# Dealing a table's tiles out over fewer edge groups in two layers of a graph network

## The chip, the cores and the metric

The program runs on one core of one Trainium2 chip. The metric is the time of one execution on the device, in microseconds (us). Three runs of the kernel before took 9591.27, 9617.38 and 9623.91 us; the median, 9617.38 us, stands for it.

## What is computed

Four layers of a graph network on 12,500 nodes of 128 features and 212,500 edges that are sorted by destination. Each layer normalises the nodes, applies a ReLU, gathers the rows of the edges' sources, combines them per destination and adds the result to x:

```python
h = relu(layernorm(x)); x = x + L0(h)   # attention over the incoming edges, GELU, layer norm
h = relu(layernorm(x)); x = x + L1(h)   # L1 = gelu(gelu(segment_sum(h[src] * w, dst)) @ W.T + b)
h = relu(layernorm(x)); x = x + L2(h)   # equivariant products per edge, summed per destination
h = relu(layernorm(x)); x = x + L3(h)   # mean of relu(h)[src] per destination, two matmuls, batch norm
```

Only layers 1 and 3 are touched by the change.

## The kernel before

Edges are cut into 208 groups of 1024: 128 partitions by T = 8 slots. For a slot, an indirect DMA on POOL's queue fetches 128 source rows, one on each partition. A one-hot matrix, made by DVE, says to which of 128 consecutive destinations each row goes, and a matmul on PE adds the rows up in PSUM. We call these eight matmuls of a group the group matmuls.

In layers 1 and 3 the destinations are split. The first 56 blocks of 128 nodes are served in this way, by the first G0 = 121 groups. The other NW = 42 blocks (windows) need no gather: the whole table of rows is loaded into SBUF once (tabS), and each window goes through NT = 26 **tiles**. A tile picks 128 rows out of the table with four matmuls by one-hot weights (out px), ACT copies px to SBUF (out xs, or xb in layer 3), and one matmul scatters them onto the window's 128 nodes (out pw). That is 42 x 26 = 1092 tiles in each of the two layers.

The tiles of layer 1 are written by the generator tabled1 (lines 1210 to 1295), those of layer 3 by tabled (from line 1465). Each resumption of the generator issues one tile; both generators have two resumptions ahead of the first tile, and that of layer 1 has one more at the end of each window. For every seven tiles or fewer the generator also issues an SP load of the tile's indices (lob) and two DVE instructions that make the one-hot matrices (oha, ohb), and for every window one small gather on POOL (xo). px has two buffers.

The order of work is written out by hand (manual_schedule). A loop counts rounds g. Round g issues on POOL the gathers of group g, on DVE its one-hot matrix, and on PE the eight group matmuls of group g - 1. After each of these eight, a formula says how many resumptions are due, and the generator is resumed until that many are done. In layer 1 (lines 1346 to 1349):

```python
goal = total * (T * (g - first) + t + 1) // (T * (last_ - first + 1))
while alive and count < min(goal, total + T + NW):
    alive = next(windows1, "end") != "end"
    count += 1
```

Layer 3 (lines 1637 to 1640) has the same formula with the limit total + T. total is 1092, first is 6 in layer 1 and 10 in layer 3, and last_ is G0 - 1 = 120 in both (lines 1311 and 1593). Rounds go on after the last group until everything else is done.

The gathered rows lie in rings: 96 buffers in layer 1 (twelve groups, line 1329), 28 in layer 3 (three and a half groups, xg). A gather waits until the group matmul that read its buffer is done.

Nodes are finished in batches of four blocks, by generators that are stepped once in a round. In layer 1 node1 (lines 603 to 624) has five steps: GELU, a matmul (L617), a bias (L620) and GELU (L621), the sum (L623) and statistics, then the normalised rows, which are stored to htab. The batch of the last gathered blocks (number 13) starts at round 123, and that of the last windows (number 24) when they are done. Layer 2 gathers from htab, so its first gather waits for the last store. In layer 3 node3 (lines 658 to 686) takes seven steps for a batch of gathered blocks and five for a batch of windows, one batch at a time; those that wait are run off after the last group. A batch norm over all nodes and the output follow.

Of the kernel before, what the change touches and what calls it, by code (L numbers as in the profile page):

```python
# [93 lines left out]
def gnn_kernel(ctx: ExitStack, tc, x, src, dst, ef16, ef9, ew, W0, We0, a0, lns, lnb, W1, b1,  # L94
# [13 lines left out]
    G0 = E * W0_ * P // (N * GE) + 2  # L108
# [15 lines left out]
    def load_edges(t, v, g0, g1, fill, k):  # L124

        full = min(g1, NF)
        if full > g0:
            nc.sync.dma_start(
                t[:, : full - g0, :],
                v[g0 * GE * k : full * GE * k].rearrange("(g p t) -> p g t", p=P, t=T * k))  # L130
        if g1 > NF:
            j, e0 = NF - g0, NF * GE
            rp, rem = divmod(tail, T)
            pool.memset(t[:, j, :], fill)
            if rp:
                nc.sync.dma_start(t[:rp, j, :], v[e0 * k : (e0 + rp * T) * k].rearrange("(p t) -> p t", t=T * k))
            if rem:
                nc.sync.dma_start(t[rp : rp + 1, j, : rem * k], v[None, (e0 + rp * T) * k : E * k])
# [464 lines left out]
    def node1(sp, pp, k, held=None):  # L603
        b0, nb = k * NBK, min(NBK, NB - k * NBK)
        xv = sp.tile([P, nb, D], F, name="xv")
        load_rows(xv, xtab[0], b0, nb)
        g = sp.tile([P, nb, P], F, name="g")
        if held is None:
            settle(k)
        act.activation(g.rearrange("p j n -> p (j n)"),  # L610
                       acc.t[:, cols(k)] if held is None else held[:, : nb * P], AF.Gelu_apprx_tanh)
        yield
        if held is None:
            vec.memset(acc.t[:, cols(k)], 0.0)
        po = pp.tile([P, nb, D], F, name="pn")
        for j in range(nb):
            pe.matmul(po[:, j, :], g[:, j, :], W1T, start=True, stop=True)  # L617
        yield
        o = sp.tile([P, nb, D], F, name="o")
        vec.tensor_tensor(o, po, b1_b[:, None, :].to_broadcast([P, nb, D]), ALU.add)  # L620
        act.activation(o, o, AF.Gelu_apprx_tanh)  # L621
        yield
        vec.tensor_tensor(xv, xv, o, ALU.add)  # L623
        yield from keep(sp, 1, k, xv, True)
# [142 lines left out]
    def gather_apart(take, table, idx):  # L767

        ts = []
        for s in range(T):  # L770
            ts.append(take())
            pool.indirect_dma_start(out=ts[-1][:, : table.shape[1]], out_offset=None, in_=table[:, :],  # L772
                                    in_offset=bass.IndirectOffsetOnAxis(ap=idx[:, s : s + 1], axis=0))
        return ts

    def one_hot(sp, r, wgt=None, dt=F):
        s = sp.tile([P, T, W], dt, name="oh")
        if wgt is None:
            vec.tensor_tensor(s, iop[:, None, :].to_broadcast([P, T, W]), r[:, :, None].to_broadcast([P, T, W]),
                              ALU.is_equal)  # L780
        else:
            for t in range(T):
                vec.tensor_scalar(s[:, t, :], io, r[:, t : t + 1], wgt[:, t : t + 1], op0=ALU.is_equal, op1=ALU.mult)
        return s
# [512 lines left out]
    with (tc.tile_pool(name="t1", bufs=1) as tp, tc.tile_pool(name="e1", bufs=3) as sp,  # L1297
          tc.tile_pool(name="e1p", bufs=2, space=PSUM) as pp,
          tc.tile_pool(name="n1", bufs=2) as ns, tc.tile_pool(name="n1p", bufs=2, space=PSUM) as np_):
        eww = tp.tile([P, NG, T], F, name="eww")  # L1300
        tabS = tp.tile([P, NB, P], F, name="tabS")
        vec.memset(tabS[:, NB - 1 :, :], 0.0)
        for g0 in (0, 16):
            load_edges(eww[:, g0 : 16 if g0 == 0 else NG, :], ew.rearrange("e o -> (e o)"), g0, 16 if g0 == 0 else NG,
                       0.0, 1)
        reg = Window(DVE, True)
        pag = pp.tile([P, 2, W], F, name="pag", bufs=1)
        S, pags, X, here, there = {}, {}, {}, [], []
        waiting = []
        windows1 = tabled1(sp, pp, tabS, lambda k, held: waiting.append((k, held)))  # L1310
        first, last_ = 6, G0 - 1
        total = NW * NT
        nk, count, alive = 0, 0, True
        with tc.manual_schedule():
            g = -1
            while g < G0 + 4 or alive or here or there or waiting:
                g += 1
                if 0 <= g - 2 < G0:
                    win = ds(reg.load(bir[0:1, g - 2 : g - 1], RW - 1), W)
                    reg.end(vec.tensor_tensor(acc.t[:, win], acc.t[:, win], pags.pop(g - 2), ALU.add))  # L1320
                if nk < W0_ // NBK and min(done[nk], G0 - 1) + 3 <= g:
                    here.append(node1(ns, np_, nk))
                    nk += 1
                if not there and waiting:
                    there = [node1(ns, np_, *waiting.pop(0))]
                here = [w for w in here if next(w, "end") != "end"]
                there = [w for w in there if next(w, "end") != "end"]
                if g < G0:
                    X[g] = gather_apart(lambda: sp.tile([P, D], F, name="X", bufs=96), htab[0], si[:, g, :])
                    S[g] = one_hot(sp, relx[:, g - G0 + GM, :] if g >= G0 - GM else rel[:, g, :], eww[:, g, :])  # L1330
                if g == 0:
                    full = NB - (LR < P)
                    for b in range(0, full, 14):
                        n = min(14, full - b)
                        nc.sync.dma_start(tabS[:, b : b + n, :],
                                          htab[0][b * P : (b + n) * P, :].rearrange("(j p) d -> p j d", p=P))
                    if full < NB:
                        nc.sync.dma_start(tabS[:LR, full, :], htab[0][full * P :, :])
                h = g - 1
                if 0 <= h < G0:  # L1340
                    p = pags[h] = pag[:, h % 2]
                    s, r = S.pop(h), X.pop(h)
                for t in range(T):
                    if 0 <= h < G0:
                        pe.matmul(p, r[t], s[:, t, :], start=t == 0, stop=t == T - 1)  # L1345
# [4 lines that stand above are left out]
# [222 lines left out]
    with tc.tile_pool(name="l3", bufs=1) as lp:  # L1572
        acc.t, acc.ring = lp.tile([P, AW], F, name="acc3"), None
        stats = lp.tile([P, NK, 6], F, name="stats")
        with (tc.tile_pool(name="t3", bufs=1) as tp, tc.tile_pool(name="e3", bufs=2) as sp,
# [14 lines left out]
            reg3 = Window(DVE, True)  # L1590
            X, S, sums, flat3, going = {}, {}, {}, {}, []
            nodes_at = [min(d, G0 - 1) + 6 for d in done[: W0_ // NBK]]
            first, last_ = 10, G0 - 1
            total = NW * NT
            with tc.manual_schedule():
                vec.memset(tabS[:, NB - 1 :, :], 0.0)
# [260 lines left out]
```

## Time and profile before

| what | value |
|---|---|
| median of three runs | 9617.38 us |
| profiled execution, its own time | 9495.71 us |
| its span in the trace | 9493.9 us |
| PE busy, share of the span | 5094.6 us, 54% |
| DVE busy | 5342.1 us, 56% |
| POOL busy | 5141.2 us, 54% |
| ACT busy | 2810.9 us, 30% |
| layer 1: first group matmul, last tile, first gather of layer 2 | at 3302.8, 5005.1, 5024.5 us |
| layer 3: first group matmul, last group matmul, last batch of nodes | at 7831.7, 9395.2, 9446 us |

The profile page gives each engine's busy time over the whole span and, in its second part, a row of 40 digits for each engine: the busy share of each fortieth of the span (237 us) in tenths. PEclk in these rows is the clock that PE was granted, in tenths of the full one. The view by stretches gives the same for any stretch of time: busy us and, in brackets, the number of instructions of each engine, then the granted clock and the DMA's share. A timeline gives single instructions in order of time: start, duration, engine, line, what it writes and reads, how many were merged, and in square brackets how long the engine was idle before and what ended that. In layer 1 a matmul in f32 shows as two instructions.

### The profile page before, as it was taken

How to read it: one execution, taken by the hardware profiler on the slowest of the kernel's cores; microseconds unless marked ns; L12 is line 12 of the kernel's file. 1: busy time of each engine (PE TensorE's matmuls, PEld its weight loads, DVE VectorE, ACT ScalarE, POOL GpSimd, SP SyncE). 2: the span in 40 equal slices, each digit the busy share in tenths (PEclk: the TensorE clock that was granted, in tenths of full speed). 3: DMA queues.
4: the chain of work that ended last, by engine and by line, in shares of the span. 5: the costliest groups of instructions: out<-in, count | busy, mean ns of one | idle time of the engine just before them, and what ended most of it. 6: DMA issues, size and time to landing. Idle time of an engine off the chain costs nothing.

```text
span 9493.9 us, 105459 instructions
## 1 busy us (share of the span) xinstructions
PE 5094.6 (54%) x33196; PEld 3216.2 (34%) x33197; DVE 5342.1 (56%) x10305; ACT 2810.9 (30%) x7511; POOL 5141.2 (54%) x5435
## 2 busy tenths in 40 slices
PE   2333333333333228888882555555555554777776
PEld 2233333333333215555551333333333331222222
DVE  4566665656657414434443777777777772444444
ACT  2232333333323303333341222222222221333333
POOL 5455555555554266666635555555555526665662
PEclk6555565555565658888896777777777776787888
DMA  6233333333333312222221112111112114333333
GB/s 119 67 77 73 73 78 73 78 75 76 75 73 74 76 51 78 76 75 76 76 67 47 49 51 55 51 52 53 52 51 55 52 41 114 86 89 85 87 89 96
DMA packets 686537, 673.64 MB, mean 71 GB/s; under 512 B 285973, under 2 KB 574088, under 8 KB 685945
## 3 DMA queue, kind: packets, MB, share of 16 engines
q0 software_dynamic: 186624, 382.17, 16.6%
q1 hardware_dynamic: 499341, 284.63, 11.6%
q8 instruction: 263, 4.31, 0.2%
q14 instruction: 309, 2.53, 0.1%
HBM read 603.91 MB, written 63.28 MB: 70 GB/s over the span
## 4 chain that ended last, share of the span: by engine, by line


## 5 line engine op out<-in xcount | busy, mean ns | idle before, releaser
L764 POOL DMA_INDIRECT X<-tab,si x1664 | 1615.7, 971 | 1411.6 <-DVE msg L1146 658.6
L764 POOL DMA_INDIRECT X<-htab,si x1664 | 1572.7, 945 | 1108.5 <-ACT prods L1386 568.8
L772 POOL DMA_INDIRECT xg<-tab,si x968 | 918.5, 949 | 650.7 <-issue 225.5
L772 POOL DMA_INDIRECT X<-htab,si x968 | 939.2, 970 | 601.0 <-PE pag L1345 233.4
L1408 PE MATMUL pag<-prods,oh 128*128 128x352 f32 x3328 | 1234.8, 533 | 0.0
L1150 PE MATMUL pag<-oh,msg 128*128 128x128 f32 x3328 | 724.7, 406 | 331.9 <-DVE msg L1146 282.8
L1408 PEld LDWEIGHTS pag<-prods,oh 128*128 128x128 f32 x3328 | 738.2, 228 | 410.3 <-issue 178.1
L1546 ACT CAST xb<-px 128x384 bf16<-128x384 f32 x1050 | 491.9, 479 | 1002.2 <-PE px L1535 374.3
L1150 PEld LDWEIGHTS pag<-oh,msg 128*128 128x128 f32 x3328 | 670.6, 308 | 347.7 <-DVE msg L1146 287.8
L1373 PE MATMUL py<-mixer,eT 72*128 72x120 f32 x416 | 131.1, 408 | 1212.4 <-ACT eT L1372 1088.0
L1282 ACT ACTIVATE xs<-px,wslot 128x128 f32<-128x128 f32 x1050 | 370.6, 366 | 1118.5 <-PE px L1270 484.1
L1070 PE MATMUL pt<-WeB,eT 128*128 128x32 f32 x416 | 123.4, 388 | 1047.9 <-ACT eT L1068 818.3
L1410 ACT COPY R<-pag 128x352 f32<-128x352 f32 x208 | 94.0, 452 | 1877.2 <-remote 1252.0
L1270 PE MATMUL px<-tabS,oha 128*32 128x128 f32 x8652 | 510.0, 310 | 236.0 <-ACT xs L1282 153.4
L1535 PE MATMUL px<-tabS,oha 128*32 128x384 bf16 x4326 | 435.1, 389 | 308.8 <-issue 213.4
L1251 PE MATMUL pw<-ohb,xs 128*128 128x128 f32 x2100 | 566.7, 355 | 13.3 <-ACT xs L1282 7.5
L1345 PE MATMUL pag<-oh,X 128*128 128x128 f32 x1936 | 437.6, 316 | 185.5 <-issue 140.0
L1373 PEld LDWEIGHTS py<-mixer,eT 72*128 72x128 f32 x416 | 82.8, 248 | 1275.1 <-ACT eT L1372 1132.3
L1386 ACT ACTIVATE prods<-X,ef 128x128 f32<-128x128 f32 x1664 | 509.6, 391 | 11.4 <-DMA X<-htab,si 11.1
L1416 DVE TENSOR_TENSOR acc<-acc,pT 128x384 f32 x208 | 114.3, 550 | 667.0 <-remote 602.2
L1070 PEld LDWEIGHTS pt<-WeB,eT 128*128 128x128 f32 x416 | 96.3, 288 | 1122.4 <-ACT eT L1068 868.3
L1139 ACT ACTIVATE oh<-iop,far 128x128 f32<-128x128 f32 x1664 | 451.6, 382 | 36.7 <-DVE ohj L982 27.7
(470 smaller groups left out, 10208.1 us busy)
## 6 DMA issues: line engine op xcount, KB each, us to landing
lob<-lo SPq DMA_DIRECT2D x252, 224.0 KB
rb<-rel SPq DMA_DIRECT2D x208, 256.0 KB
X<-htab,si POOLq DMA_INDIRECT x2632
X<-tab,si POOLq DMA_INDIRECT x1664
xtab<-xv SPq DMA_DIRECT2D x72, 256.0 KB
xv<-xtab SPq DMA_DIRECT2D x72, 256.0 KB
xg<-tab,si POOLq DMA_INDIRECT x968
lob<-lo SPq DMA_DIRECT2D x84, 160.0 KB
```

The costliest lines, as they stand in the source:

```text
L764: pool.indirect_dma_start(out=t[:, s, :], out_offset=None, in_=table[:, :], in_offset=bass.IndirectOffsetOnAxis(ap=idx[:, s : s + 1], axis=0))
L772: pool.indirect_dma_start(out=ts[-1][:, : table.shape[1]], out_offset=None, in_=table[:, :], in_offset=bass.IndirectOffsetOnAxis(ap=idx[:, ...
L1139: act.activation(S[:, t, :], iop, AF.Abs, bias=far[:, t : t + 1])
L1150: pe.matmul(pag, msg[:, t, :], S[:, t, :], start=t == 0, stop=t == T - 1)
L1251: pe.matmul(pw, x, b, start=j == 0, stop=j == NT - 1)
L1270: pe.matmul(px[q * SL : (q + 1) * SL, :], a[:, jj * P + q * SL : jj * P + (q + 1) * SL], tabS[:, blk, :], start=True, stop=True)
L1282: act.activation(x, px, AF.Copy, scale=by)
L1345: pe.matmul(p, r[t], s[:, t, :], start=t == 0, stop=t == T - 1)
L1386: act.activation(A[:, t, :], X[:, t, :], AF.Copy, scale=e[:, t, 0:1])
L1408: pe.matmul(pag, S[:, t, :], prods[:, t, :], start=t == 0, stop=t == T - 1)
L1535: pe.matmul(px[q * SL : (q + 1) * SL, :], a[:, jj * P + q * SL : jj * P + (q + 1) * SL], tabS[:, blk, :], start=True, stop=True)
L1546: act.copy(x[:, : 3 * P], px)
```

## The change

The last round by which the formula has all 1092 resumptions due is moved four rounds ahead, in both layers:

```diff
-        first, last_ = 6, G0 - 1
+        first, last_ = 6, G0 - 5
...
-            first, last_ = 10, G0 - 1
+            first, last_ = 10, G0 - 5
```

last_ is 116 in place of 120. Nothing else differs: the same instructions on the same data, with the tiles in another place among the groups.

## The prediction

> **What bounds the kernel now.** I read the page's rows of slices first, for the stretches of layers 1 and 3 and for what PE does when POOL stops in each.
>
> ```profile
> PE   2333333333333228888882555555555554777776
> POOL 5455555555554266666635555555555526665662
> PEclk6555565555565658888896777777777776787888
> ```
>
> Layer 1 is slices 15 to 21, layer 3 the last seven. PE is busiest in both; at the end of each POOL falls to nothing and PE's clock rises. Next the view by stretches: a middle and an end without gathers for layer 1, the same for layer 3.
>
> ```profile
> 4200.00:4850.00 650.00, 522.83 (x5314) 340.22 (x5313) 262.85 (x728) 214.46 (x567) 402.82 (x414) 0.88 0.29 77
> 4862.00:4962.00 100.00, 97.18 (x1161) 65.20 (x1162) 56.95 (x160) 51.13 (x130) 0.00 (x0) 1.00 0.20 57
> 8000.00:9360.00 1360.00, 1007.15 (x6587) 310.30 (x6586) 585.05 (x1165) 517.46 (x1103) 831.96 (x880) 0.81 0.33 87
> 9376.00:9391.00 15.00, 15.00 (x126) 4.77 (x126) 7.81 (x15) 9.56 (x20) 0.00 (x0) 0.99 0.01 2
> ```
>
> While POOL gathers, PE is 80% busy at clock 0.88 (layer 1) and 74% at 0.81 (layer 3); without gathers it is full at 1.00. So a tile costs more beside gathers. How much work goes through, by the same view for the scatter matmul alone:
>
> ```profile
> 4300.00:4400.00 100.00, 37.25 (x141) 23.23 (x142) 0.90 0.29 77
> 4862.00:4962.00 100.00, 47.03 (x198) 29.23 (x198) 1.00 0.20 57
> ...
> 9200.00:9300.00 100.00, 28.27 (x75) 7.25 (x75) 0.85 0.32 87
> 9376.00:9391.00 15.00, 6.75 (x20) 1.92 (x20) 0.99 0.01 2
> ```
>
> In layer 1 (two matmuls a tile) 70 tiles in 100 us beside gathers, 99 without; in layer 3 75, and 20 in 15 us, or 133. The waits say why PE is short of full: beside gathers ACT's copy xs waits for PE for 401 us over 420 times, up to 3.4 us at a time, though ACT is a third busy; without gathers the same wait is 93 times 0.6 us. Something in the gathers holds signals back, 1 to 2 us now and then, and PE with two px buffers stands still. The gathers themselves are not the bound: POOL waits for PE to free buffers (pag 214 us in layer 1, pg 217 us in layer 3), and counting gathers against group matmuls in the timeline, POOL is always its whole ring ahead, 12 groups or 3.3 to 3.5. **PE is the bound in both layers, slowed by gathers.**
>
> **The change, counted.** Resumptions a round rise from 1092/115 = 9.50 to 1092/111 = 9.84 in layer 1, and from 1092/111 = 9.84 to 1092/107 = 10.21 in layer 3. Nothing is added or removed; no wait is new. With the tiles move ACT's copies, DVE's oha and ohb (0.69 and 1.09 us for seven tiles), SP's lob loads and POOL's xo gather (one for 26 tiles). DVE at 43% and 40%, ACT at 33% and 38% and DMA at 0.29 and 0.33 cover 4% more of that; if they did not, the tiles would just keep waiting as they do.
>
> Layer 1 does not do what the change says. Its generator needs 2 + 1092 + 42 + 1 = 1137 resumptions and its limit lets the goal run past 1092. They end in round 125 (958 x 1092/920 = 1137) before, in round 121 (925 x 1092/888) after: just inside the last group's matmuls. No group gets PE alone; what goes is the stretch of tiles behind the last group. In layer 3 the 1097 or so resumptions end in round 121 before and 117 after, so groups 116 to 120 do stand alone.
>
> **Layer 1.** The end now, from the timelines of PE, DVE and POOL:
>
> ```profile
> 4970.61 0.39 PE L1345 MATMUL pag<-oh,X 128*128 128x128 f32 x2
> ...
> 5005.14 0.49 PE L1251 MATMUL pw<-ohb,xs 128*128 128x128 f32 x2
> ```
> ```profile
> 5010.74 5.50 DVE L1448 MEMSET acc<- 128x6528 f32 x1 [1.84 <-ACT t L557]
> 5016.16 0.36 DVE L620 TENSOR_TENSOR o<-pn,b_b 128x256 f32<-128x256 f32 x1
> ```
> ```profile
> 5024.53 0.96 POOL L764 DMA_INDIRECT X<-htab,si  x1 [33.92 <-DMA htab<-t]
> ```
>
> Behind the last group matmul come 34.5 us with 34 tiles, node batch 13's matmul (1.9 us), idle gaps of 0.3, 1.5 and 0.8 us and 10.2 us at half clock. Then 19.4 us for batch 24 until layer 2 gathers, 5.5 us of it layer 2's memset ahead of the batch's L620 on DVE.
>
> After: the 34 tiles go ahead of the last group, and since the ring is 12 groups long they land beside gathers (round 110 has 36 resumptions more behind it). Price of one: at least 0.77 us, the pitch of tiles with no gather (4971.70, 4972.47, ...). At most 1.34 us: between two group matmuls in the gathering stretch a step with one tile takes 1.41 us (mean of 537) and one with two 2.75 (111); without gathers 1.04 and 1.85. In between stands the ratio of throughputs, 0.77 x 99/70 = 1.09. Stalls only come within 2 us of a gather's start, and the number of gathers is the same, which speaks for the lower end; the step means speak for the upper. I take 0.95. The last group then ends at 4970.6 + 34 x 0.95 = 5002.9 (4996.8 to 5016.2), and PE is done with it, not at 5005.1.
>
> The tail behind it is new: batches 13 and 24 both start in rounds 122 and 123 and go side by side. Batch 13's chain from its rows: accumulation 0.3, GELU table and GELU 1.3 + 0.6, matmul 1.2, L620 0.7, GELU 0.6, sum and statistics 1.9, square root with its table 1.6, L547 and L550 1.3, ReLU 1.0, store until the gather 2.7: 13.2, with ten hops of 0.15 14.7. Batch 24's shorter instructions get between for 2 to 3 us: 17.5. The memset adds 5.5 if it lies in the chain again; it waited for batch 13's ReLU, which is now last, and then it hides under the 9 us before layer 2's first products. I take 18, from 15 to 23. Layer 2 starts at 5002.9 + 18 = 5020.9: **3.6 us early** (5011.8 to 5039.2: 13 early to 15 late).
>
> **Layer 3.** PE reaches group 116 at 9347.3 and its last group matmul at 9395.2, 47.9 us later, with 44 tiles in between:
>
> ```profile
> 9367.44 0.95 POOL L772 DMA_INDIRECT xg<-tab,si  x1 [0.30 <-DMA lob<-lo]
> ```
> ```profile
> 9394.58 0.98 PE L1636 MATMUL pg<-xg,oh 128*128 128x385 bf16 x5
> ```
>
> After, 39 tiles more precede group 116 (goal 1093 in place of 1054 there). Price: 0.545 us at full clock (pitch of two tiles in one step) to 1.01 (2.09 less 1.08, steps with two tiles and one), by throughput 0.545 x 133/75 = 0.97; at the stretch's clock 0.81 the lower one becomes 0.65. I take 0.72, nearer to it since PE alone gives it: 28.1 us. From there PE has eight matmuls of 0.17 us a group and runs into the gathers: of 968, the ring lets 956 go before group 116 is read, and 12 are left at 1.25 us (0.95 and 0.30 to issue). The last starts 13.8 us in, lands 2.6 us later (first gather of layer 2: 5024.53, used at 5027.12): 17 us. So 28.1 + 17 = 45.1 against 47.9: 2.8 us early. POOL, not PE, is late next. The batch of nodes in rounds 120 to 126 holds DVE for 3.35 us (reciprocal, L669) just behind the last group now, ahead of L1607; after, it falls into the wait for gathers: 2 us more. The batches behind are one at a time in either kernel and were always queued, so those 46 us stay. **4.8 us early** (21.3 + 15 - 47.9 - 3 = 15 early; 39.4 + 17 - 47.9 = 8.5 late).
>
> A row on the clock: half at 4983.28 after gaps of 0.3 and 1.5 us, and L681 takes 2.07 us at 9403 where it takes 1.12 at 9419. The Trainium skill (TensorE: Matmul & The Clock Gate, Part 1: The HAM clock gate) says that PE falls to half clock after an idle window of about 3.4 us and is freed after a busy one, and so speaks against leaving PE sparse groups. The trace shows the half clock, after shorter gaps. By that rule layer 3's sparse groups run cold, which the 1.25 us between gathers hides, and the first two node batches, which are cold today already; a third would add 1.9 us.
>
> **The sum.** 3.6 + 4.8 = 8.4 us less. The profiled execution took 9495.7 us (span 9493.9 and 1.8 around it): 9487.3 after, a share of 0.9991. The runs' median is 1.3% above that execution; 0.9991 x 9617.4 = 9609.
>
> **Rivals.**
> 1. *The moved tiles pay the full price of gathers* (slower). Price 1.34 and 1.01 us a tile: 34 x 0.39 = 13 and 39 x 0.29 = 11 more than I took, so 16 us more than before: 9633; with the memset in the chain, 9639. For it: the step means. Against: the gathers are no more than before. It decides in layer 3 from (47.9 - 17)/39 = 0.79 us a tile, in layer 1 from (5024.5 - 18 - 4970.6)/34 = 1.06.
> 2. *The moved tiles cost what they cost alone.* 0.77 and 0.545: 28 us less with both tails at their best: 9589. For it: stalls stop 2 us behind a gather. Against: each tile also adds a copy that must be signalled.
> 3. *Nothing of it shows*: layer 1 keeps no group clear, and layer 3 trades PE's wait for POOL's: 9617.
>
> The rest is left for a scheduler that orders instructions elsewhere differently.
>
> **The numbers.** About 0.3%, 29 us, is what a measurement of this kernel can tell from no change. Forecast with rival 3: 0.46. Rival 1: 0.28, of which 0.15 beyond 29 us with the scatter of the runs, which lie 33 us apart. Rival 2: 0.14, half of it beyond. The rest, 0.12, a third each way. So faster 0.07 + 0.04 = 0.11, same 0.46 + 0.13 + 0.07 + 0.04 = 0.70, slower 0.15 + 0.04 = 0.19. Range 9575 to 9650: the rivals' 9589 and 9639 and 12 us of scatter of the runs.
>
> **What would show it.** Right: the last group matmul of layer 1 near 5003 with no tiles behind it; layer 2's first gather 0 to 10 us sooner; in layer 3 a gap-ridden PE from group 116 on, with L1636 waiting for the xg gathers, and 65 us or so from there to the last batch. Wrong: tiles of 1.3 us or more beside gathers in both layers, or a POOL that is no longer its whole ring ahead.

## The result and the profile after

The kernel after takes 9557.15 us (median of 20 runs, 9532.23 to 9586.81), the kernel before 9591.38 us in the 20 runs beside it (9568.22 to 9623.91). The ratio is **0.9961, with an interval of 0.9952 to 0.9970**: 37 us less, 29 to 46. The forecast was 9609, 8 us less, in a range from 9575 up; the direction was right and the size was not. Of the 52 us between forecast and measurement, 26 lie in the time before (9591 in these 20 runs, 9617 in the prediction's three) and 26 in the change.

The same program takes 7,212 to 7,252 us on some occasions and 9,476 to 9,624 us on others; the result and the prediction's profile are of the longer kind and most experiments of the shorter, so each experiment is compared only with its own runs of the kernel before.

The two profiled executions can't be subtracted. That of before took 9495.71 us, less than any of its 20 runs above; that of after took 9562.19 us, 66 us more, although the kernel is faster. Layer 0, which is the same in both, already ends 35 us later (layer 1's first gather: 3298.0 before, 3333.1 after). So I read stretches within each. First the rows of slices of the page of after.

```profile
PE   2333333333333328888883555555555564777776
POOL 5455555555544266556635555555555526665663
PEclk6565565555555658888886777777777786888887
```

They look as before. By the view by stretches (busy us and number of PE, PEld, DVE, ACT, POOL, then granted clock, DMA share, GB/s): a middle and the end of layer 1's groups, then layer 3's middle and its end.

```profile
4250.00:4900.00 650.00, 533.74 (x5353) 348.16 (x5349) 261.41 (x724) 218.95 (x571) 392.57 (x401) 0.85 0.28 76
4945.00:5045.00 100.00, 94.64 (x1100) 63.23 (x1104) 56.17 (x160) 47.94 (x123) 0.20 (x1) 0.98 0.17 52
8065.00:9425.00 1360.00, 1010.63 (x6662) 313.42 (x6662) 586.23 (x1169) 527.90 (x1125) 819.47 (x867) 0.82 0.32 86
9440.00:9464.00 24.00, 18.14 (x67) 7.20 (x66) 13.88 (x32) 1.94 (x4) 10.40 (x11) 0.73 0.18 50
```

Beside gathers PE is 82% busy in layer 1 (80% before) and 74% in layer 3 (74%). Layer 3's end is now a sparse PE beside eleven gathers, where PE was alone and full before.

What ends layer 1, by the timelines of PE, DVE and POOL of after:

```profile
5057.33 0.39 PE L1251 MATMUL pw<-ohb,xs 128*128 128x128 f32 x2
5057.56 1.06 PE L1345 MATMUL pag<-oh,X 128*128 128x128 f32 x8
```
```profile
5061.23 5.50 DVE L1448 MEMSET acc<- 128x6528 f32 x1 [2.29 <-ACT g L610]
5066.78 0.48 DVE L614 MEMSET acc<- 128x512 f32 x1
5067.19 0.96 DVE L620 TENSOR_TENSOR o<-pn,b_b 128x256 f32<-128x256 f32 x2
```
```profile
5078.03 0.95 POOL L764 DMA_INDIRECT X<-htab,si  x1 [45.98 <-DMA htab<-t]
```

The last tile (L1251) is now just ahead of the last group matmul (L1345, the last one of the merged eight at 5058.3), where it was 34.6 us behind it. From the last group matmul to layer 2's first gather it takes 19.7 us; before it took 5024.5 - 4970.7 = 53.8. The stretch is **34.1 us shorter**. DVE's memset for layer 2 lies in the chain again: L614 and L620 of the last batches stand behind it.

Layer 3's end by the timelines of POOL and PE of after:

```profile
9454.40 0.95 POOL L772 DMA_INDIRECT xg<-tab,si  x1 [0.30 <-issue]
```
```profile
9454.26 1.48 PE L1636 MATMUL pg<-xg,oh 128*128 128x385 bf16 x8 [0.50 <-DVE oh L779]
9459.34 0.33 PE L1644 MATMUL pm<-ident,f 128*128 128x128 f32 x1 [3.60 <-DVE acc L1614]
9460.53 2.75 PE L1636 MATMUL pg<-xg,oh 128*128 128x385 bf16 x8
```

The last tile starts at 9441.6, and the last group matmul at 9462.8. PE waits for the gathers, and ahead of the last group for DVE: the last gather starts at 9454.4, but L1644, which waits for DVE's L1614, runs only at 9459.3, and the last eight matmuls stand behind it. From group 116's first matmul it takes 25.1 us (47.9 before, with 44 tiles in it), but 39 tiles more lie ahead of it. What those cost is read further down, where more profiles have layer 3 in the old order.

### The profile page after: what moved, and what is told of

Its sections match the earlier page's. It is cut to its first block, busy times and chain, and to the rows that moved or that the text cites. A ratio compares the mean times of both kernels' runs of the same rounds, so it can differ in the third digit from the quotient of the medians.

```text
span 9560.4 us, 105476 instructions
## 1 busy us (share of the span) xinstructions
PE 5140.1 (54%) x33196; PEld 3252.8 (34%) x33197; DVE 5345.9 (56%) x10305; ACT 2807.2 (29%) x7509; POOL 5145.5 (54%) x5435
## 5 line engine op out<-in xcount | busy, mean ns | idle before, releaser
L1251 PE MATMUL pw<-ohb,xs 128*128 128x128 f32 x2100 | 579.7, 362 | 24.1 <-ACT xs L1282 21.4
L1345 PE MATMUL pag<-oh,X 128*128 128x128 f32 x1936 | 445.0, 320 | 189.5 <-issue 145.1
```

Source lines behind the costliest of these rows:

```text
L1251: pe.matmul(pw, x, b, start=j == 0, stop=j == NT - 1)
```

## The experiments

**Each layer alone.** Two kernels have the change in one layer only, and the kernels before and after ran once beside them, for a second profile.

```diff
 l1_only
+        first, last_ = 6, G0 - 5
...
             first, last_ = 10, G0 - 1
 l3_only
         first, last_ = 6, G0 - 1
...
+            first, last_ = 10, G0 - 5
```

> Layer 1 alone has last_ = G0 - 5; layer 3 is as before. The whole change measured 0.9961 of the time before (0.9952 to 0.9970), 37 us, where the prediction had 3.6 us from layer 1 and 4.8 us from layer 3. Theory A (layer 1 carries the gain: its 34 tiles behind the last group were dear, and the two last node batches now share one tail): 0.9965 to 0.9980 here, 20 to 35 us. Theory B (layer 3 carries it: the moved tiles are nearly free beside gathers): 0.9990 to 1.0005 here. If each layer gives half: about 0.998.

> Layer 3 alone has last_ = G0 - 5; layer 1 is as before. Theory A: 0.9990 to 1.0005. Theory B: 0.9963 to 0.9980, 20 to 35 us, with the time from group 116's first matmul to the last group matmul down from 48 us to 25 or less and the groups before it hardly slower. If each layer gives half: about 0.998.

> The kernel before once more, for a second profile. The two single profiles (9493.9 us before, 9560.4 us after) differ the other way than the medians of 20 runs do, and mostly in layers 0 and 2 that the change does not touch. A second profile of before shows how far the same stage moves between executions: by either theory layer 0 should vary by some 20 to 40 us, and layers 1 and 3 by 10 to 25.

> The changed kernel once more, for a second profile. Theory A: layer 1 (first gather to layer 2's first gather) is 20 to 35 us shorter than in the second profile of before. Theory B: layer 3 (first gather to the last batch's statistics) is.

Measured beside before's 7230.48 us: layer 1 alone 7202.74, a ratio of 0.9959 [0.9946, 0.9973]; layer 3 alone 1.0008 [0.9998, 1.0017]; single runs of before and after, 7242.5 and 7195.01 us. So the gain is layer 1's, and layer 3 gives none here. These executions are shorter than the prediction's profile by a quarter, and the trace shows another balance. The view by stretches of before_copy, layer 1's middle, and a row of POOL's waits in the same stretch (us in total, times, longest):

```profile
2700.00:3550.00 850.00, 782.54 (x8586) 519.29 (x8586) 425.07 (x1189) 355.25 (x913) 648.49 (x662) 0.94 0.34 94
```
```profile
POOL X L772 <- PE pag L1345: 37.2, 122, 0.3
```

PE is 92% busy at clock 0.94, and POOL never waits over 0.3 us for a buffer: it issues one gather after another, 1.25 us apart, and is only 0.4 to 0.6 groups ahead of PE (12 in the prediction's profile). Eight gathers a round and the windows' own, 8.36 x 1.25 = 10.5 us, are nearly the round's 10.7. Here gathers set the pace, and moved tiles lie beside them.

Layer 3 shows it at its end. The last tile starts 45.9 us ahead of the last group matmul in after_copy (7051.4 to 7097.3) in place of 5.7 us in before_copy (7128.2 to 7133.9). Yet the last xg gather starts 2.6 us ahead of it in both, straight behind the one before, by the POOL timelines of before_copy and after_copy:

```profile
7131.30 0.95 POOL L772 DMA_INDIRECT xg<-tab,si  x1 [0.30 <-issue]
```
```profile
7094.64 0.95 POOL L772 DMA_INDIRECT xg<-tab,si  x1 [0.30 <-issue]
```

The gathers end last, with the tiles out of the way or not; from group 116 to the last group matmul it takes 49.2 and 48.3 us.

**More of it, and the memset elsewhere.** l1_m9 has the tiles due eight rounds earlier in layer 1; l1_pool is l1_only with layer 2's memset on POOL. The two of above went along again.

```diff
 l1_m9
+        first, last_ = 6, G0 - 9
 l1_pool
+        first, last_ = 6, G0 - 5
...
-            vec.memset(acc.t, 0.0)
+            pool.memset(acc.t, 0.0)
```

> Layer 1's edit alone, again. The first trial ran on a chip on which the kernel before takes 7230 us (the runs of the prediction: 9591) and gave 0.9959, 30 us, with the 34.6 us of tiles behind the last group gone and no more time before it. Theory A2 (a tile beside gathers is free because the gathers set the pace there): 25 to 35 us again if signals come on time; where signals come late (ACT's copy waits 0.37 us on average in place of 0.10), PE sets the pace and the same edit gives 0 to 15 us. Theory A3 (the moved tiles are nearly free there too, because a late signal costs the same whatever is queued): 25 to 35 us on either chip.

> Layer 3's edit alone, again; the first trial gave 1.0008 (0.9998 to 1.0017). Theory A2: within 5 us of before where signals come on time, since 12 gathers are left at 1.25 us when PE reaches group 117 in either kernel; where they come late, 0 to 10 us less. Theory A3: 10 to 20 us less where they come late.

> Layer 1 with last_ = G0 - 9, layer 3 as before: the tiles end four rounds before the last group. If the gain is the stretch of tiles behind the last group and nothing else, there is none left to win: within 5 us of layer 1's edit alone, at most 3 us better because the last windows' batch is done before the last group ends. If denser tiles cost PE time beside gathers: 5 to 15 us worse than layer 1's edit alone.

> Layer 1's edit alone, and layer 2's memset of its accumulators (L1448, 5.5 us) on POOL in place of DVE. In both kernels the memset stands on DVE ahead of the last node batch's bias (L620), and layer 2's first gather waits for that batch's store; POOL is idle there for 15 us. If it is in the chain: 4 to 6 us better than layer 1's edit alone, with layer 2's first gather 16 us behind the last group matmul in place of 21 to 22. If the store or the square root's table is late next: no better.

Measured beside 7227.66 us: l1_only_2 0.9953 [0.9939, 0.9966], l3_only_2 1.0003 [0.9992, 1.0014], l1_m9 0.9955 [0.9941, 0.9969], l1_pool 0.9941 [0.9928, 0.9954]. The end of layer 1 with the old order, from PE's and POOL's timelines of l3_only_2:

```profile
3683.80 0.39 PE L1345 MATMUL pag<-oh,X 128*128 128x128 f32 x2
...
3718.34 0.49 PE L1251 MATMUL pw<-ohb,xs 128*128 128x128 f32 x2
```
```profile
3680.27 0.95 POOL L772 DMA_INDIRECT X<-htab,si  x1 [0.30 <-issue]
...
3737.74 0.96 POOL L764 DMA_INDIRECT X<-htab,si  x1 [33.13 <-DMA htab<-t]
```

and with the new one, from those of l1_only_2:

```profile
3682.83 0.39 PE L1251 MATMUL pw<-ohb,xs 128*128 128x128 f32 x2
...
3685.40 0.49 PE L1345 MATMUL pag<-oh,X 128*128 128x128 f32 x2 [0.80 <-DMA X<-htab,si]
```
```profile
3682.90 0.94 POOL L772 DMA_INDIRECT X<-htab,si  x1 [0.30 <-DMA X<-htab,si]
3704.59 0.95 POOL L764 DMA_INDIRECT X<-htab,si  x1 [20.52 <-DMA htab<-t]
```

In both the last group matmul follows the last gather by some 3 us, and in l1_only_2 it waits for that gather's DMA. With the old order 34.6 us of tiles come behind, and then 19.2 us until layer 2's first gather; with the new one 19.0 us is all. What the tiles cost where they now lie: from the first matmul of group 16 to that of group 109 it takes 993.7 us in l3_only_2 and 993.9 in l1_only_2, with 9.50 and 9.84 resumptions a round, 32 more in all. The six profiles of the shorter kind with the old order lie between 991.9 and 1000.3 us (mean 996.4), the eight with last_ = G0 - 5 between 993.9 and 1001.8 (997.9). That is 1.5 us for 32 resumptions, well within the scatter: **next to nothing**. The middle of l1_only_2, in the view by stretches, shows where they went:

```profile
2700.00:3550.00 850.00, 789.25 (x8879) 523.86 (x8877) 435.00 (x1203) 370.47 (x952) 647.78 (x664) 0.96 0.35 95
```

Beside the row of before_copy above, PE does 293 matmul instructions more in 7 us more of busy time, at clock 0.96 in place of 0.94, beside 664 POOL instructions in place of 662.

l1_m9 ends the tiles 43.7 us ahead of the last group matmul and gains nothing over l1_only. Groups 16 to 109 take 1002.3 us, and from group 16 to the last group matmul it takes 1124.5, within the 1118.7 to 1127.8 of the eight. From there to layer 2's first gather it takes 24.0 us, 5 more than in l1_only_2: DVE's memset (at 3689.44) now stands ahead of the last windows' L547 and L550, and batch 13's GELU (L610, at 3698.54) behind these on ACT. Once the tiles are not last, more room brings no more, and here it put the memset in a worse place.

l1_pool's POOL timeline:

```profile
3692.91 5.54 POOL L1448 MEMSET acc<- 128x6528 f32 x1 [1.98 <-PE pag L1345]
3705.30 0.95 POOL L764 DMA_INDIRECT X<-htab,si  x1 [6.86 <-DMA htab<-t]
```

The memset takes as long on POOL as on DVE, but lies beside the last batches. From the last group matmul to layer 2's first gather it takes 12.9 us in place of 19.0: the memset's 5.5 us were in the chain.

**Two more pairs and a whole set.** The same kernels again, to narrow the intervals.

> Layer 1's edit alone, a third time, to meet a chip like the prediction's, on which the kernel before takes 9500 to 9600 us and signals come late beside gathers. There: theory A2 (PE sets the pace beside gathers, a moved tile costs 0.77 us or more) 0.9985 to 1.000; theory A3 (a moved tile is nearly free there too) 0.9965 to 0.9975. On a chip of 7230 us both say 0.9955 once more.

> Layer 3's edit alone, a third time. On a chip of 9500 to 9600 us: theory A2 0.999 to 1.000; theory A3 0.998 to 0.999, so that both layers together give the 0.9961 that was measured there. On a chip of 7230 us: within 0.1% of before.

> Layer 1's edit alone. On a chip with late signals: price of a moved tile as forecast (0.95 us) 0.999 to 1.000; price near 0.25 us (a third of what it costs alone, as for the doubled px matmuls) 0.9970 to 0.9985. On a chip of 7230 us 0.9955.

> Layer 3's edit alone. On a chip with late signals: price as forecast (0.72 us) 0.999 to 1.000; price near 0.2 us: 47.9 us become 8 + 17, 20 to 25 us less, 0.9974 to 0.9985. On a chip of 7230 us 1.000.

> Both edits, the whole change. On a chip with late signals 0.996 again, and the sum of the two edits. On a chip of 7230 us as layer 1 alone, 0.9955.

> Layer 1's edit and layer 2's memset on POOL: 4 to 6 us less than layer 1's edit alone on either chip.

Measured: beside 7227.18 us l1_only_3 0.9951 [0.9934, 0.9969] and l3_only_3 1.0001 [0.9990, 1.0011]; beside 7231.13 us l1_only_4 0.9954 [0.9938, 0.9969], l3_only_4 1.0006 [0.9994, 1.0017], after_4 0.9961 [0.9949, 0.9974], l1_pool_2 0.9937 [0.9922, 0.9952]. Layer 1 alone gains as much as the whole change. l1_pool is the best version: 7190.86 and 7187.49 us, 5 and 7 us below l1_only of the same occasion and 18 below after_4, though its interval touches those of its neighbours.

**Is PE the bound beside gathers?** The prediction says so; then work added to PE in layer 1 has to be paid. pe2_before and pe2_l1 are the kernel before and l1_only with the four px matmuls of every tile of layer 1 issued twice. The second four write the same values.

```diff
-                    for q in range(4):
+                    for q in (0, 1, 2, 3, 0, 1, 2, 3):
```

> The kernel before with the four px matmuls of each tile of layer 1 issued twice, on the same data, to make PE the slowest engine there: some 0.36 us more for a tile, 9.5 tiles a round, so a round of 12.8 us of PE against 10.7 us of gathers. By every theory 150 to 260 us more than before, POOL's ring full (12 groups ahead) and about 45 to 50 us of tiles behind the last group.

> The same with layer 1's last_ = G0 - 5; to be read against the run just before it. Theory A2 (the gain exists only where the gathers set the pace; where PE does, the moved tiles are paid in full): 0 to 12 us less than with last_ = G0 - 1, from the idle gaps and the shared tail alone. Theory A3 (moved tiles are free beside gathers whoever sets the pace): 35 to 50 us less.

These fell on an occasion of the longer kind, like that of the prediction's profile: before 9489.24 us. The chip has the number 10 in the record, as it has for the sets with 7227.66 and 7227.18 us, so the expectations' "chip of 7230 us" is no property of the chip. pe2_before takes 9557.34, a ratio of 1.0078 [1.0064, 1.0092], and pe2_l1 9553.2, 1.0070 [1.0057, 1.0084]. Where no gathers run, four px matmuls more cost 0.19 us a tile (groups 109 to the last take 132.6 us in place of 111.7, with 110 or so tiles). For 1092 tiles that is 207 us, and 68 were paid: 0.062 us a tile, **a third**, where the expectation had 150 to 260 us by every theory; the tiles behind the last group take 36.9 us in place of its 45 to 50. The rows of layer 1's middle, of pe2_before and then of pe2_l1:

```profile
3550.00:4800.00 1250.00, 1077.45 (x16482) 769.99 (x16486) 492.72 (x1366) 396.05 (x1053) 733.34 (x762) 0.97 0.27 74
```
```profile
3550.00:4800.00 1250.00, 1079.09 (x16869) 775.06 (x16862) 495.65 (x1359) 408.31 (x1080) 726.94 (x756) 0.98 0.27 74
```

PE's busy share rises from 80% to 86% and its granted clock from 0.88 to 0.97, while POOL is still its whole ring of twelve groups ahead. In groups 16 to 109, with 850 tiles, the work added is 162 us at 0.19 a tile. Beside the profile of before, the stretch is 52 us longer (1225.7 to 1277.9), PE is idle for 51 us less (228 to 177), and its busy time is only 103 us more (998 to 1101): the other 59 went in the faster clock. So idle time, clock and time paid took about a third each.

The pair against each other was to tell what moved tiles cost on a PE with less room. Its medians differ by 4 us, with an interval of some 13 us either way: that fits theory A2's 0 to 12 us, and theory A3's 35 to 50 lie outside it. In the traces the stretch from layer 1's first gather to layer 2's is 22 us shorter in pe2_l1 (1810.6 to 1788.6), where its tail behind the last group matmul alone is 36 us shorter (56.1 to 19.7). So on a PE with this load a moved tile is not free: some 0.4 us by the traces, 0.9 by the medians.

**Layer 1 alone where the time is the longer one, and layer 3 once more.**

> Layer 1's edit alone. On a chip with late signals: price of a moved tile as forecast (0.95 us) 0.999 to 1.000; price near 0.25 us 0.9970 to 0.9985, and layer 3 then has 0 to 20 us. On a chip of 7230 us 0.9955 once more.

> Layer 3's edit alone. On a chip with late signals: if the two edits add up to the whole change, 0.9990 (5 to 15 us less); if layer 1 is all of it, 1.000; with a moved tile at 0.2 us, 0.9974 to 0.9985. On a chip of 7230 us 1.000.

l1_only_5 takes 9546.95 us beside 9574.6, a ratio of 0.9971 [0.9959, 0.9983]: 28 us less, 16 to 39. That is outside what the expectation had for the forecast's price of 0.95 us and inside its range for 0.25, but the interval reaches further on both sides. l3_only_5 fell on an occasion of the shorter kind: 0.9999 [0.9990, 1.0008] beside 7231.39. So the layer-1 half was measured in both kinds, the layer-3 half in the shorter one only. The middle of l1_only_5's layer 1:

```profile
3560.00:4800.00 1240.00, 1003.97 (x10242) 656.92 (x10242) 498.41 (x1373) 417.31 (x1094) 745.70 (x768) 0.87 0.27 75
```

PE is 81% busy at clock 0.87, near the 80% at 0.88 and the 82% at 0.85 in the middles of before and after, and not at the 92% of the shorter occasions.

No trace shows the 28 us. The tail behind the last group matmul is 19.7 us, as in after, and 53.8 in before. But groups 16 to 109 take 1257.7 us in l1_only_5, 1263.5 in after and 1225.7 in before, so that by these three a resumption more would cost 1.0 to 1.2 us. They are not of one occasion: before's profiled execution is over 70 us shorter than the fastest of its 20 runs, and layers 0 and 2, which are the same in all, are 23 and 13 us shorter in it than in l1_only_5. There is no profile of the kernel before, with its px work single, on an occasion of l1_only_5's kind. So on the longer occasions the gain of layer 1 rests on the times of whole runs.

For layer 3, four profiles of the longer kind have the old order (before, l1_only_5, pe2_before, pe2_l1) and one, after, the new one. From its first gather to group 116 the four take 1515.5 to 1528.1 us and after 1547.3: 39 tiles cost 19 to 32 us there, **0.5 to 0.8 us each**. From the first gather to the last group matmul the four take 1561.4 to 1577.2 us and after 1572.4: no gain shows.

## Why the prediction was wrong, point by point

- **"PE is the bound in both layers, slowed by gathers": as a ground for charging a moved tile in full, this step failed in layer 1.** It rested on POOL being a whole ring ahead. The ring says that PE's group matmuls are late, not that PE's work makes them late: PE was 80% busy in the same rows, and with the px work doubled only a third of it was paid. PE, for which POOL waits, was itself waiting a fifth of the time. On the shorter occasions gathers set the pace. In layer 3 on the longer ones no run tested the step, and there the one profile of the new order charges the tiles about as forecast.
- **The price of a moved tile in layer 1, 0.95 us between 0.77 and 1.34: mis-sized, with a wrong lower end. This is the term that failed.** On the shorter occasions it is 1.5 us for 32 resumptions. On the longer ones the runs of l1_only_5 give (53.8 - 19.7 - 28)/34 = 0.2 us, from -0.2 to 0.5 by their interval. At 0.95 the change would have gained 2 us there, and at 0.77, the lower end, 8. The prediction had named an 80% busy PE and, for the lower end, gathers whose number stays the same; both told that a tile could lie in time that is lost anyway, and the lower end had to be 0. Rival 2 had the direction, with a price still too high. Against the 0.2 us stand the profiles of different occasions, with 1 us or more, and the pair with doubled px work, with 0.4 to 0.9; only a profile of the kernel before on the occasion of its runs would settle it.
- **Why the tiles cost so little on the longer occasions is argued, not shown.** Beside gathers (groups 16 to 109) ACT's copy xs starts 1.1 us (mean) after the end of its px matmuls in before, 1.0 in after and 1.1 in l1_only_5, which have more tiles; where no gathers run it is 0.3 us in before, and on the shorter occasions 0.2 in both (the expectations' 0.37 and 0.10 are lower than this). If this lateness hangs on the gathers, whose number is the same, then more tiles fill it up and don't add to it. That stalls come within 2 us of a gather's start, which the prediction took for a sign, tells nothing: in the same groups of before 97% of the tiles' px matmuls, on time or not, end within 2 us of one. No run without gathers was made; it would change the whole layer.
- **Layer 1's tiles end in round 121, inside the last group, and no group gets PE alone: right.** l1_m9, which does give the last groups a PE alone, brings no more.
- **The tail of two batches side by side, 18 us from 15 to 23: right, by luck**, 19.7 in after, 19.0 in l1_only_2. "Then it hides", of the memset, was wrong: it stands ahead of L614 and L620, and 6 us go when it is on POOL. Without it the tail is 12.9 us, where the prediction had 17.5. Two errors of 5 and 6 us cancelled.
- **Layer 3, 4.8 us early: no gain shows.** "POOL, not PE, is late next" is what the traces of before_copy and after_copy show, and there the change gives nothing in five comparisons, 0.9999 to 1.0008. On the longer occasions 37 us for the whole and 28 for layer 1 alone leave 9, but the intervals overlap, and the trace of after shows none. Its price, 0.5 to 0.8 us a tile, is near the 0.72 of the forecast.
- **The 17 us from group 116 to the end became 25.1.** The last gather started at 9454.4, 16.7 us in, and not 13.8: ahead of it POOL had stood still up to 2.06 us at a time for PE's group matmuls. Then DVE's chain for the group before (L1607 to L1614) held PE for 3.60 us ahead of L1644, and the last eight matmuls ran at half clock, 2.75 us in place of 1.48. The batches behind stayed: 51.4 us before, 49.9 after.
- **The rule on the clock.** The sparse groups ran cold in part, as the prediction put the rule to. By the view by stretches of after:

```profile
9436.00:9441.90 5.90, 5.02 (x22) 1.38 (x21) 1.89 (x5) 2.80 (x7) 2.76 (x4) 0.50 0.18 54
9443.30:9449.50 6.20, 6.17 (x13) 2.46 (x14) 3.26 (x10) 0.00 (x0) 3.88 (x5) 0.50 0.22 63
```

  Here the half clock came behind idle gaps of 0.3, 0.7 and 2.2 us, in PE's timeline of after from 9426. From 9449.6 on the clock was full, and L1636's eight take 1.48 us at 9454.26 behind a gap of 0.50 us; behind the one of 3.60 us it was half again, and they take 2.75. The Trainium skill (TensorE: Matmul & The Clock Gate, Part 1: The HAM clock gate) names an idle window of about 3.4 us. The trace agrees at the second place and not at the first.
- **The sum.** In layer 1, 34 us of the stretch were there to be had. The forecast took 32 of them back as the price of the moved tiles; the runs of layer 1 alone took back 6.

## What to carry to other kernels

A full ring of buffers tells who is late, not what makes it late. Before extra work is charged in full to an engine that is 80% busy, put a known amount of extra work on it and see what share is paid; until then the lower end of its price is zero. In layer 1, work that stood alone behind the last transfer of its stage was worth most of its length ahead of it (28 of 34 us by the runs), and moving it further brought nothing; in layer 3 the same move brought nothing that shows. Take the profiles of before and after on the same occasion, or a stage's share of a small gain can't be read from them.

## What the runs showed of the hardware

- The same program took 7,230 us on some occasions and 9,490 to 9,590 on others, without any difference in the kernel, and both on the chip with the number 10; layer 2's memset and the gathers take the same in both (5.50 us, 0.95 us). Beside gathers in layer 1, ACT's copies start 1.1 us after PE's matmuls on the longer ones and 0.2 us on the shorter. Why is open.
- PE's granted clock in layer 1's middle rose from 0.88 to 0.97 when its work was doubled in part, and a px matmul instruction took 285 ns on average in place of 314: some of the added work is paid by the clock.
- PE fell to half clock at 9436 us of after with no idle gap over 2.2 us in the 10 us before, and at 4983 us of before behind gaps of 0.3 and 1.5 us.
- A memset of 128 x 6528 in f32 takes 5.54 us on POOL and 5.50 on DVE.
